# Windowed attention: weighted values by features, softmax weights divided on POOL, transposes in four groups, masks of 32 rows

## The chip, the core and the metric

The kernel runs on one core of a Trainium2 chip. Its engines work side by side, each on its own queue of instructions: TensorE (PE) multiplies matrices and loads their stationary operands (PEld), VectorE (DVE) and ScalarE (ACT) do element work and read TensorE's results from PSUM, GpSimd (POOL) does element work on SBUF only, and SyncE (SP) starts the DMAs. The metric is the device time of one execution in microseconds, the median of several runs.

## The reference

The input is x of 8 batches of 512 rows and 128 features. A first stage adds to x a normed linear attention (16 heads, squared scores). The second stage, which the change touches, runs six layers of windowed attention and a feed-forward block on the normed x. Cut to what matters:

```python
for i in range(6):
    x = attn_layer(shift_tokens(x), Wqkv[i], q_scale[i], k_scale[i], Wo[i]) + x
    x = ffn_layer(shift_tokens(x), ln_g[i], ln_b[i], W1[i], b1[i], W2[i], b2[i]) + x

def attn_layer(x, Wqkv, qs, ksc, Wo):          # 16 heads of 64
    q, k, v = split(x @ Wqkv, 3)
    q = rotate(l2norm(q) * qs); k = rotate(l2norm(k) * ksc)
    # windows of 32 rows: each row sees its window and the one before it
    sim = bq @ [bk_prev, bk].T * 8, masked
    out = softmax(sim) @ [bv_prev, bv]
    return out @ Wo
```

All data is float32. The masks are bfloat16.

## The kernel before, in words

The 512 rows of a batch are four blocks of 128 rows, each with four windows of 32. A block of a batch in a layer is a *unit*; there are 6 x 8 x 4 = 192. The state of a batch lies in SBUF by features (`state[b]`, 128 features by rows).

The loop over t is a software pipeline: in slot t, unit t is projected, unit t-1 gets its scores, unit t-2 its weighted values, and unit t-3 its output product. The feed-forward block of a batch follows its last block (j = 3) at lags 3 to 6, so the slots with t mod 4 = 2, 3, 0 and 1 hold the norm's transposes (`feed_norm`), the normed transposes (`feed_first`), the hidden layer (`feed_middle`) and the last product (`feed_last`).

The steps of a unit:

- `proj(s)`, s = 0 for q and 1 for k (L409): two matmuls of 512 columns (each runs in two passes) into a PSUM tile `mm` of two banks. DVE multiplies them by the rotary tables (L429 twice, L436), ACT squares them (L444), POOL adds the two products into `qk` (L454), DVE sums the squares per head (L457). `unit_length` makes the inverse root on ACT and multiplies q and k by it on POOL (L470).
- `values` (L474): v's projection into an `mm` tile, copied by ACT (L482); SP's DMAs then bring each window's own and previous 32 rows side by side into `v2`.
- `by_features` (L498): transposes of q and k, two calls of eight (four of q, four of k), into `tr` tiles of one bank each, copied by ACT into `qT` and `kT` (L514). POOL keeps k's last 32 columns for the next block (L517).
- `scores` (L519): two matmuls write the mask into the two banks of `sp` (L527), 64 products of 64 rows by 32 columns add q times k (L534). DVE takes the maximum (L542), ACT sixteen exponentials into `pe` (L546), DVE the sum and its reciprocal (L552, L553).
- `by_keys` (L556): transposes of `pe`, copied by ACT into `pT` (L564).
- `weigh_values` (L566): 64 products with `pT` as the stationary operand (64 rows by 32 columns) and 64 columns of v streamed, into `po` (L574). DVE divides by the sum on the way out, `on` (L582).
- `out_by_features` (L588): eight transposes of `on`, two ACT copies into `oT` (L596). `out_project` (L598): eight products with Wo (L603), which DVE adds to the state (L608).

TensorE runs in the order in which the code issues its work (`manual_schedule` at L694). On the other engines a planner orders the instructions from the code's order, its own costs and `high_priority` marks; `issue_behind(later, earlier)` forces an order on one engine without a wait. PSUM is rotated: `mm` has two buffers of two banks, `tr` two of one bank, and `s` has a single buffer of two banks which `sp` and `po` share in turn. A matmul into a rotated buffer waits for the readers of its previous content.

ACT loads the gelu table at the start of a slot with a hidden layer, behind the previous exponentials (L81), and the table of logarithm and exponential behind the last gelu (L75).

Of the kernel before, what the change touches and what calls it, by code (L numbers as in the profile page):

```python
# [26 lines left out]
def sandwich_kernel(ctx: ExitStack, tc: tile.TileContext, ins: dict, out: bass.AP):  # L27
# [40 lines left out]

    def transposed(ps, src, rows, cols):
        nc.tensor.transpose(ps[:cols, :rows], src, ident[:rows, :rows])  # L70


    tables, exps, divisions = [], [], []
# [7 lines left out]
    def gelu_only():  # L81
        ld = nc.scalar.preload_act_table_set("gelu_and_others")
        issue_behind(ld, exps[-1])
        tables.append(ld)
# [324 lines left out]
    def proj(u, s):  # L409
# [18 lines left out]
        def turned(a):  # L428
            nc.vector.tensor_tensor(  # L429
# [4 lines left out]

        def straight():
            nc.vector.tensor_tensor(  # L436
# [6 lines left out]
        def squared(a):  # L443
            nc.scalar.activation(sq[:, :, a, :], ps[:, a], AF.Square)  # L444

# [3 lines left out]
        squared(0)  # L449
        squared(1)  # L450
        u["sq"] = sq
        if s == 0:
            sum_squares(u, 0)
        nc.gpsimd.tensor_tensor(qk[:, s].rearrange("p h a d -> p a h d"), t1, t2, ALU.add)  # L454

    def sum_squares(u, s):
        su = nc.vector.tensor_reduce(  # L457
            u["ss"][:, s], u["sq"].rearrange("p h a d -> p h (a d)"), AX.X, ALU.add
        )
        if s == 1 and divisions:  # L460
            issue_behind(su, divisions[-1])
# [12 lines left out]
    def values(u):  # L474
# [3 lines left out]
        v0 = f3.tile([P, 2, 512], F32, tag="v0", name="v0")  # L478
        ps = psum.tile([P, 2, 512], F32, tag="mm", name="mm")
        for p in range(2):  # L480
            nc.tensor.matmul(ps[:, p, :], lhs, L["wqkv"][:, 2, p, :], start=True, stop=True)  # L481
        nc.scalar.copy(v0, ps)  # L482
# [15 lines left out]
    def by_features(u, c):  # L498

        j, qk, B_ = u["j"], u["qk"], u["B"]  # L500
        if c == 0:
            u["qT"] = f1.tile([P, NP, P], F32, tag="qT", name="qT")
            if j == 0:
# [3 lines left out]
        for s in range(2):  # L507
            ps = psum.tile([P, 4, P], F32, tag="tr", name="tr")
            for i in range(4):
                h0 = 2 * (c + i)  # L510
                transposed(ps[:, i, :], qk[:, s, h0 : h0 + 2].rearrange("p h a d -> p (h a d)"), P, P)
            dst = u["qT"][:, c : c + 4, :] if s == 0 else u["kT"][:, c : c + 4, W:]
            with tc.high_priority():
                nc.scalar.copy(dst, ps)  # L514
        if c == NP - 4 and j < NB - 1:
# [3 lines left out]
    def scores(u):  # L519
# [4 lines left out]
        mk = mask0 if u["j"] == 0 else mask  # L524
        sp = psum.tile([P, 2, NP, 2 * W], F32, tag="s", name="sp", bufs=1)
        for p in range(2):
            nc.tensor.matmul(  # L527
                sp[:, p], identb, mk.unsqueeze(1).to_broadcast([P, NP, 2 * W]),
# [22 lines left out]
        su = f2.tile([P, NP, 2], F32, tag="su", name="su")  # L551
        nc.vector.tensor_reduce(su, pe, AX.X, ALU.add)  # L552
        nc.vector.reciprocal(su, su)  # L553
        u["pe"], u["su"] = pe, su

    def by_keys(u):  # L556
        pe = u["pe"]
        u["pT"] = pT = f1.tile([P, NP, P], F32, tag="pT", name="pT")
        for c in range(0, NP, 4):
# [3 lines left out]
            with tc.high_priority():  # L563
                nc.scalar.copy(pT[:, c : c + 4, :], ps)  # L564

    def weigh_values(u):  # L566

        v2, pT, su = u["v2"], u["pT"], u["su"]
        po = psum.tile([P, 2, NP, HD], F32, tag="s", name="po", bufs=1)
        for pair in range(NP):  # L570
            for w in range(4):
                for p in range(2):
                    r = slice(HD * p, HD * (p + 1))
                    nc.tensor.matmul(  # L574
                        po[W * w : W * (w + 1), p, pair, :],
                        pT[r, pair, W * w : W * (w + 1)],
                        v2[r, w, HD * pair : HD * (pair + 1)],
                        start=True, stop=True,
                    )
# [251 lines left out]
```

## Time and profile before

| | |
|---|---|
| median of 3 runs | 3899.24 us (3893.05 to 3900.62) |
| the profiled execution | 3893.85 us |
| its span, first to last instruction | 3892.1 us |
| first stage (before the first slot of the loop over t) | about 535 us of the span |
| PE busy, mean granted clock | 3729.8 us (96%), 0.99 |
| DVE, ACT, POOL busy | 72%, 68%, 47% |
| DMA, mean share of 16 engines by queue | 22.4% + 0.9% + 0.1% |

A line of the page's groups reads: line of the kernel, engine, operation, output <- inputs, shape, count | busy us, mean ns of one | idle before it and what ended it. A line in order of time reads: start us, duration us, engine, line, operation, how many merged, and in brackets the idle time before it and its releaser. A line by windows reads: the window and its length, then for each engine the busy us and the number of instructions, the granted TensorE clock, the DMA share and GB/s. PE durations include the pipeline's latency, so starts, not durations, give the rate of matmuls.

### The profile page before, as it was taken

What the parts mean: (1) busy time and instruction counts of PE and PEld (TensorE: products, weight loads), DVE (VectorE), ACT (ScalarE), POOL (GpSimd) and SP (SyncE); (2) the same over time, 40 slices, a digit from 0 to 9 for tenths busy, and PEclk for the clock granted to TensorE, in tenths of its full rate; (3) what the DMA queues carried; (4) which work ended last, traced back from release to release, by engine and by line L of the source; (5) the groups of instructions that cost most, each with busy time, mean ns of one, the idle gap of its engine ahead of it and who ended that gap; (6) DMA issues with size and microseconds to landing.
All of it is one profiled execution on the core that took longest, in us unless ns stands there. A gap on an engine that the chain in (4) does not pass through costs nothing.

```text
span 3892.1 us, 149565 instructions
## 1 busy us (share of the span) xinstructions
PE 3729.8 (96%) x65600; PEld 2474.2 (64%) x65600; DVE 2818.2 (72%) x4300; ACT 2657.5 (68%) x6745; POOL 1837.0 (47%) x1311
## 2 busy tenths in 40 slices
PE   8999989999999999999999999999999999999997
PEld 4555456666666666666666666666666666666665
DVE  4555567777867777777777777777787777777775
ACT  5565656776767777777777677777677777766664
POOL 0000025555555555555555555555555555555552
PEclk9999999999999999999999999999999999999998
DMA  2000012222222222222222322223222222222221
GB/s 81 17 9 12 6 50 71 59 66 60 76 74 63 63 63 66 71 75 65 60 62 64 82 65 66 65 56 82 70 66 59 66 65 56 65 68 68 64 67 37
DMA packets 153208, 233.46 MB, mean 60 GB/s; under 512 B 32622, under 2 KB 53356, under 8 KB 151788
## 3 DMA queue, kind: packets, MB, share of 16 engines
q1 hardware_dynamic: 152556, 223.89, 22.4%
q8 instruction: 517, 8.47, 0.9%
q14 instruction: 135, 1.11, 0.1%
HBM read 24.54 MB, written 4.19 MB: 7 GB/s over the span
## 4 chain that ended last, share of the span: by engine, by line
PE 89%; ACT 5%; issue 3%; DVE 2%; DMA 0%; POOL 0%; POOLq 0%; DVEq 0%; SPq 0%; ACTq 0%
PE tr L70 17%; PE mm L421 17%; PE mm L481 9%; PE py L603 9%; PE sp L534 7%; PE po L574 6%; PE y L282 4%; PE mm L625 3%; PE py L657 3%; PE mm L626 3%; PE sc L252 2%; PE sp L527 2%; ACT sq L444 2%; PE vv L230 2%; PE po L318 2%
## 5 line engine op out<-in xcount | busy, mean ns | idle before, releaser
L454 POOL TENSOR_TENSOR qk<-t,t 128x1024 f32<-128x1024 f32 x384 | 909.2, 2368 | 999.6 <-DVE t L436 999.5
L421 PE MATMUL mm<-wqkv,state 128*128 128x512 f32 x1536 | 727.1, 596 | 3.7 <-ACT v L482 2.6
L470 POOL TENSOR_TENSOR qk<-qk,ss 128x1024 f32<-128x1024 f32 x384 | 722.3, 1902 | 16.0
L429 DVE TENSOR_TENSOR t<-mm,tab 128x512 f32<-128x512 f32 x768 | 497.8, 685 | 242.8 <-PE mm L421 231.3
L546 ACT ACTIVATE pe<-sp,mx 128x64 f32<-128x64 f32 x3072 | 651.4, 376 | 27.6 <-DVE mx L542 27.3
L436 DVE TENSOR_TENSOR t<-mm,tab 128x1024 f32<-128x1024 f32 x384 | 465.9, 1213 | 0.0
L457 DVE TENSOR_REDUCE ss<-sq 128x16 f32<-128x1024 f32 x384 | 461.9, 1203 | 2.0 <-ACT sq L444 2.0
L444 ACT ACTIVATE sq<-mm 128x512 f32<-128x512 f32 x768 | 422.6, 610 | 47.2 <-DVE t L436 45.6
L603 PEld LDWEIGHTS py<-oT,wo 128*128 128x128 f32 x3072 | 374.8, 193 | 93.5 <-issue 56.2
L70 PEld LDWEIGHTS tr<-ident,qk 128*128 128x128 f32 x3072 | 345.7, 141 | 127.1 <-issue 105.7
L70 PE MATMUL tr<-ident,qk 128*128 128x128 f32 x3072 | 412.1, 277 | 7.4 <-ACT qT L514 2.3
L596 ACT COPY oT<-tr 128x512 f32<-128x512 f32 x384 | 207.3, 589 | 266.2 <-PE tr L70 265.2
L421 PEld LDWEIGHTS mm<-wqkv,state 128*128 128x128 f32 x1536 | 264.1, 192 | 191.6 <-issue 188.0
L481 PE MATMUL mm<-wqkv,state 128*128 128x512 f32 x768 | 367.9, 602 | 16.8 <-ACT sq L444 16.8
L603 PE MATMUL py<-oT,wo 128*128 128x128 f32 x3072 | 376.0, 276 | 1.0 <-ACT oT L596 0.9
L582 DVE TENSOR_TENSOR on<-po,su 128x1024 f32<-128x1024 f32 x192 | 235.1, 1224 | 170.1 <-PE po L574 170.1
L534 PEld LDWEIGHTS sp<-kT,qT 64*32 64x32 f32 x24576 | 271.9, 106 | 116.7 <-issue 113.8
L574 PE MATMUL po<-v,pT 64*32 64x64 f32 x24576 | 299.3, 225 | 44.7 <-issue 44.7
L482 ACT COPY v<-mm 128x1024 f32<-128x1024 f32 x192 | 194.5, 1013 | 211.0 <-PE mm L481 211.0
L534 PE MATMUL sp<-kT,qT 64*32 64x64 f32 x24576 | 312.2, 227 | 26.0 <-issue 25.2
L574 PEld LDWEIGHTS po<-v,pT 64*32 64x32 f32 x24576 | 258.5, 105 | 86.4 <-issue 86.2
L542 DVE TENSOR_REDUCE mx<-sp 128x16 f32<-128x1024 f32 x192 | 234.6, 1222 | 106.9 <-PE sp L534 106.3
(108 smaller groups left out, 5171.0 us busy)
## 6 DMA issues: line engine op xcount, KB each, us to landing
v<-v SPq DMA_DIRECT2D x1152, 128.0 KB
v<-v SPq DMA_DIRECT2D x672, 64.0 KB
wqkv<-in_L_ffn_Wqkv_dram SPq DMA_DIRECT2D x6, 1536.0 KB
wo<-in_L_ffn_Wo_dram SPq DMA_DIRECT2D x6, 512.0 KB
xin<-_attn_hidden_states_dram SPq DMA_DIRECT2D x8, 256.0 KB
xr<-_attn_hidden_states_dram SPq DMA_DIRECT2D x8, 256.0 KB
x<-xr SPq DMA_DIRECT2D x8, 256.0 KB
xr<-x SPq DMA_DIRECT2D x8, 256.0 KB
```

The lines of the kernel that those rows point to most:

```text
L70: nc.tensor.transpose(ps[:cols, :rows], src, ident[:rows, :rows])
L421: nc.tensor.matmul(ps[:, a].rearrange("p h d -> p (h d)"), lhs, wqkv[:, s, a, :], start=True, stop=True)
L429: nc.vector.tensor_tensor(t2[:, a], ps[:, 1 - a], tab[:, 2 * s + 1, j, HF * a : HF * (a + 1)].unsqueeze(1).to_broadcast([P, H, HF]), ALU.mult,
L436: nc.vector.tensor_tensor(t1, ps, tab[:, 2 * s, j, :].rearrange("p (a d) -> p a d", a=2).unsqueeze(2) .to_broadcast([P, 2, H, HF]), ALU.mult,)
L444: nc.scalar.activation(sq[:, :, a, :], ps[:, a], AF.Square)
L454: nc.gpsimd.tensor_tensor(qk[:, s].rearrange("p h a d -> p a h d"), t1, t2, ALU.add)
L470: nc.gpsimd.tensor_tensor(t, t, ss[:, i, :].unsqueeze(2).to_broadcast([P, H, HD]), ALU.mult)
L481: nc.tensor.matmul(ps[:, p, :], lhs, L["wqkv"][:, 2, p, :], start=True, stop=True)
L534: nc.tensor.matmul(sp[W * w : W * (w + 1), p, pair, :], qT[HD * p : HD * (p + 1), pair, W * w : W * (w + 1)], kT[HD * p : HD * (p + 1), pa ...
L546: ex = nc.scalar.activation(pe[:, pair, p, :], sp[:, p, pair, :], AF.Exp, bias=mx[:, p, pair : pair + 1])
L574: nc.tensor.matmul(po[W * w : W * (w + 1), p, pair, :], pT[r, pair, W * w : W * (w + 1)], v2[r, w, HD * pair : HD * (pair + 1)], start=Tru ...
L603: nc.tensor.matmul(py, L["wo"][:, c, :], oT[:, c, :], start=(c == 0), stop=(c == NP - 1))
```

## The change

Four things change in the second stage.

1. *Weighted values by features.* In `weigh_values` v is now the stationary operand (64 rows by 64 columns) and 32 columns of `pT` are streamed, so the result comes out with features on the partitions. The transposes and copies of `out_by_features` go; one ACT copy of 128 x 1024 makes `oT`. The rows of Wo are put into the matching order before the launch.
2. *Division on POOL.* A new step `shares`, two slots behind the projection, sums the exponentials in two halves on DVE and multiplies the weights themselves by the reciprocals on POOL, before `by_keys` transposes them.
3. *Order.* `by_features` now does four transposes per call, of q or of k; the first two calls come ahead of `values`, `by_keys` comes after it, the third call before `weigh_values` and the fourth after. `values` is issued in halves, of which ACT copies one and DVE the other. Squares, sums of squares and additions become steps of their own, and new `issue_behind` edges order them: the first squares behind the exponentials, q's and k's copies behind the first squares, the second squares behind q's second copy, the second projection's products behind the half sums, the additions behind the division. The gelu table is loaded behind the copies of `by_keys`.
4. *Masks of 32 rows.* For all but a batch's first block, the mask product takes 32 rows, with a fourfold identity `each` as the stationary operand; the two banks' products use different rows of the array.

```diff
+    each = const.tile([2 * W, P], BF16, tag="each", name="each")
+    for a in range(2):
+        for w in range(4):
+            nc.vector.tensor_copy(
+                each[W * a : W * (a + 1), W * w : W * (w + 1)], ident[W * a : W * (a + 1), W * a : W * (a + 1)]
+            )
...
-        issue_behind(ld, exps[-1])
+        issue_behind(ld, pcopies[-1])
...
+            if s == 1 and sums:
+                issue_behind(t, sums[-1])
...
-        squared(0)
-        squared(1)
...
+    def squared(u, s):
+        sq, ps = u["sq", s], u.pop(("psum", s))
+        for a in range(2):
+            q2 = nc.scalar.activation(sq[:, :, a, :], ps[:, a], AF.Square)
+            if s == 0 and exps:
+                issue_behind(q2, exps[-1])
+            if s == 1 and "cp" in u:
+                issue_behind(q2, u["cp"])
         if s == 0:
-            sum_squares(u, 0)
-        nc.gpsimd.tensor_tensor(qk[:, s].rearrange("p h a d -> p a h d"), t1, t2, ALU.add)
+            qsquares.append(q2)
+
+    def add_turned(u, s):
+        t1, t2 = u.pop("parts")
+        add = nc.gpsimd.tensor_tensor(u["qk"][:, s].rearrange("p h a d -> p a h d"), t1, t2, ALU.add)
+        if divisions:
+            issue_behind(add, divisions[-1])
...
-        if s == 1 and divisions:
-            issue_behind(su, divisions[-1])
+        if s == 0:
+            issue_behind(su, u["straight"])
...
-        for p in range(2):
-            nc.tensor.matmul(ps[:, p, :], lhs, L["wqkv"][:, 2, p, :], start=True, stop=True)
-        nc.scalar.copy(v0, ps)
+        nc.tensor.matmul(ps[:, half, :], lhs, L["wqkv"][:, 2, half, :], start=True, stop=True)
+        if half == 0:
+            nc.scalar.copy(v0[:, 0], ps[:, 0])
+            return
+        nc.vector.tensor_copy(v0[:, 1], ps[:, 1])
...
+        with tc.high_priority():
+            cp = nc.scalar.copy(dst, ps)
+        issue_behind(cp, qsquares[-1])
+        u["cp"] = cp
...
+            r = slice(W * p, W * (p + 1))
+            lhs, mk = (identb, mask0) if u["j"] == 0 else (each[r], mask[r])
             nc.tensor.matmul(
-                sp[:, p], identb, mk.unsqueeze(1).to_broadcast([P, NP, 2 * W]),
+                sp[:, p], lhs, mk.unsqueeze(1).to_broadcast([lhs.shape[0], NP, 2 * W]),
...
-        su = f2.tile([P, NP, 2], F32, tag="su", name="su")
-        nc.vector.tensor_reduce(su, pe, AX.X, ALU.add)
-        nc.vector.reciprocal(su, su)
...
+    def shares(u):
+
+        pe = u["pe"]
+        for c in range(0, NP, 4):
+            part = pe[:, c : c + 4].rearrange("t c p k -> t (c p) k")
+            su = f2.tile([P, NP], F32, tag=f"su{c}", name="su")
+            red = nc.vector.tensor_reduce(su, part, AX.X, ALU.add)
+            if sums:
+                issue_behind(red, sums[-1])
+            rc = nc.vector.reciprocal(su, su)
+            sums.append(rc)
+            with tc.high_priority():
+                dv = nc.gpsimd.tensor_tensor(
+                    part, part, su.unsqueeze(2).to_broadcast([P, NP, 2 * W]), ALU.mult
+                )
+        divisions.append(dv)
...
-        po = psum.tile([P, 2, NP, HD], F32, tag="s", name="po", bufs=1)
-        for pair in range(NP):
+        po = psum.tile([P, 2, NP // 2, P], F32, tag="s", name="po", bufs=1)
+        for k in range(NP // 2):
             for w in range(4):
...
+                for i in range(2):
+                    for p in range(2):
+                        r, c, o = slice(HD * p, HD * (p + 1)), 2 * k + i, HD * (i ^ p)
+                        nc.tensor.matmul(
+                            po[o : o + HD, p, k, W * w : W * (w + 1)],
+                            v2[r, w, HD * c : HD * (c + 1)],
+                            pT[r, c, W * w : W * (w + 1)],
+                            start=True, stop=True, skip_group_check=True,
+                        )
+        u["oT"] = oT = f1.tile([P, 2, NP // 2, P], F32, tag="oT", name="oT")
         with tc.high_priority():
...
+            nc.scalar.copy(oT, po)
...
+            at(t, 0, proj, 0)
+            at(t, 3, out_project)
+            at(t, 0, squared, 0)
+            at(t, 2, shares)
+            at(t, 0, add_turned, 0)
+            at(t, 0, proj, 1)
+            at(t, 0, add_turned, 1)
+            at(t, 0, sum_squares, 0)
...
+            at(t, 1, by_features, 0, 0)
+            at(t, 1, by_features, 0, 1)
+            at(t, 0, values, 0)
+            at(t, 0, values, 1)
+            at(t, 2, by_keys)
             if gelus:
                 gelu_only()
...
+            at(t, 1, by_features, 4, 0)
+            if 0 < t < len(units):
+                units[t]["cp"] = units[t - 1]["cp"]
+            at(t, 0, squared, 1)
             at(t, 2, weigh_values)
             at(t, 0, sum_squares, 1)
             if not gelus:
                 at(t, 0, unit_length)
-            at(t, 1, by_features, 4)
+            at(t, 1, by_features, 4, 1)
...
-            at(t, 2, out_by_features)
```

## The prediction

> **What bounds the kernel now.** I read the page first (busy shares and the chain that ended last), then the busy time slot by slot, then one slot in order of time. "Slot" is one turn of the loop over t; its start is the first matmul of `proj(0)`. From the page, the shares and the chain:
>
> ```profile
> PE 3729.8 (96%) x65600; PEld 2474.2 (64%) x65600; DVE 2818.2 (72%) x4300; ACT 2657.5 (68%) x6745; POOL 1837.0 (47%) x1311
> PE 89%; ACT 5%; issue 3%; DVE 2%; DMA 0%; POOL 0%; POOLq 0%; DVEq 0%; SPq 0%; ACTq 0%
> ```
>
> TensorE is the bound and its waits are few. Busy time in four slots in a row, t mod 4 = 0, 1, 2, 3 (window, length, engines):
>
> ```profile
> 2168.59:2189.37 20.78, 20.78 (x331) 12.80 (x331) 13.53 (x18) 15.45 (x37) 7.30 (x7) 0.92 0.23 59
> 2189.37:2206.84 17.47, 16.82 (x326) 11.40 (x325) 12.74 (x17) 11.05 (x32) 12.34 (x9) 1.00 0.16 40
> 2206.84:2221.43 14.59, 14.59 (x325) 10.76 (x323) 12.09 (x23) 11.45 (x34) 7.11 (x6) 1.00 0.38 99
> 2221.43:2238.05 16.62, 15.32 (x324) 10.97 (x323) 13.96 (x20) 11.15 (x32) 9.73 (x7) 1.00 0.26 65
> ```
>
> Over the 48 slots of each kind the medians between starts are 19.81, 16.77, 14.87 and 15.73 us: they differ by the feed-forward piece (hidden layer, last product, transposes of the norm, of the normed). 192 slots fill 3275 of the 3892 us. The third slot in order of time (start, duration, what):
>
> ```profile
> 2206.19 1.23 DVE L542 TENSOR_REDUCE mx<-sp 128x16 f32<-128x1024 f32 x1 [0.61 <-PE sp L534]
> 2207.56 3.39 ACT L546 ACTIVATE pe<-sp,mx 128x64 f32<-128x64 f32 x16
> ...
> 2210.04 1.21 DVE L436 TENSOR_TENSOR t<-mm,tab 128x1024 f32<-128x1024 f32 x1
> ...
> 2211.34 1.09 ACT L444 ACTIVATE sq<-mm 128x512 f32<-128x512 f32 x2 [0.39 <-DVE t L436]
> ...
> 2212.06 1.04 PE L70 MATMUL tr<-ident,pe 128*128 128x128 f32 x8
> ...
> 2212.70 1.08 ACT L564 COPY pT<-tr 128x512 f32<-128x512 f32 x2 [0.27 <-PE tr L70]
> ...
> 2215.62 1.49 PE L574 MATMUL po<-v,pT 64*32 64x64 f32 x128
> ...
> 2217.14 1.23 DVE L582 TENSOR_TENSOR on<-po,su 128x1024 f32<-128x1024 f32 x1 [0.41 <-PE po L574]
> ...
> 2218.42 0.59 PE L527 MATMUL sp<-mask,identb 128*128 128x512 bf16 x2
> ...
> 2218.95 1.62 PE L534 MATMUL sp<-kT,qT 64*32 64x64 f32 x128
> ...
> 2220.50 1.09 PE L70 MATMUL tr<-ident,on 128*128 128x128 f32 x8
> ```
>
> The reader should see TensorE's pieces lying end to end, and two facts that matter below: the division (`on`) of 1.23 us lies under eight transposes and the norm's before the masks reuse its PSUM banks, and the last eight transposes (2220.50) stand between the scores and the next slot, so that the maximum and the start of the exponentials lie under them.
>
> **What the Trainium skill says.** "TensorE: Matmul & The Clock Gate", section LDWEIGHTS: a load costs its columns over 1.2 ns, rows do not count; 64 columns are 53 ns. The trace agrees: in the sums L212 (N=4, so only the loads matter) sixteen pairs of 128 columns start 0.112 us apart. "TensorEngine Tiling (Array Packing)", Key Properties: different tiles load and multiply in parallel, a change of mode drains. The trace agrees: L252 records eight 128-column loads in 0.42 us, where in turn they would take 0.89. "PSUM — Partial Sum Buffer", Terms: two engines may not be on one bank at once, reads included. So squares follow the DVE products of the same projection: the 0.39 us wait at 2211.34.
>
> ```profile
> 94.05 1.95 PE L212 MATMUL vs<-cb,tw 128*128 128x4 f32 x16 [0.16 <-ACT tqk L222]
> ...
> 319.26 0.42 PEld L252 LDWEIGHTS sc<-tqk 32*128 32x128 f32 x8
> ```
>
> **The change part by part**, per slot, starts read from the third slot.
> - Output transposes go: eight at 0.109 us, 0.87 us of TensorE, and two ACT copies of 0.59; one ACT copy of 128x1024 comes (`v` L482: 1.01 us).
> - Masks of 32 rows: two 0.216 us matmuls in separate row groups run together: -0.22 us, in three slots of four (first blocks keep the old mask).
> - Weighing: still 128 loads and 128 matmuls, but loads of 64 columns on four tiles instead of 32 columns on eight. Now: 1.27 us at best (start 2215.62, last about 1.27 later), 1.42 to the next piece. After: half of 0.112 is 0.056 us per load and tile, 32 rounds = 1.79 us; +0.5. Bounds: 1.27 (loads hide) and 2.64 if a tile can't load while it multiplies (0.056+0.027, 32 rounds). I take 1.79: in the old burst eight tiles issue in 0.056 us with a 64-column matmul each, so loads hide there.
> - Division leaves DVE (1.23) for POOL: two multiplies of 128x512, each half of L470's 1.90, say 1.0. Two half sums (0.68 each, as L429's 512 elements) and two reciprocals replace 1.22+0.24. POOL goes from about 9.1 to 11.1 us per slot; cover: it is idle after its two unit-length multiplies, which now end about 3.5 us into the next slot, while the q transposes want them at 5.2. After the feed-forward slot it is about 5.1 against 5.66 for k.
> - Half of v's copy moves to DVE, +0.68: DVE stays at 12 of 14.6 us, cover.
> - New orders, and what queues behind: on ACT behind the first squares the q and k copies and half of v's; on DVE behind the half sums the second projection's products (from 6.7; today from 7.48) and then `sum_squares`; on POOL behind the division both additions, 7.95 to 12.7, then the unit length.
> - Eight small copies for `each` at the start and Wo in another row order (same bytes): nothing; the input loads cover them.
> - SP's ten or so v DMAs wait for the later weighing (about 1.4 us later) and for DVE's half copy; their tile is read two slots on: nothing.
>
> Now the order. Times from the slot's start, which is now the end of the scores: projections and `out_project` to 5.22 as now; four groups less two: q, k 5.22 to 6.10; values to 7.82; `by_keys` to 8.75.
> Upstream: maximum 0.1 to 1.32, exponentials 1.5 to 4.84, first squares (put behind them) 4.8 to 5.9; values need that bank pair at 6.10: slack about 0.2. Half sums follow the state adds, 4.94 to 6.65, POOL 5.9 to 6.95 and 6.95 to 7.95; `by_keys`' second half wants it at 8.3: slack 0.3.
> Downstream, where the gain is lost: the second q group reuses the `tr` buffer of `by_keys`' first half, whose copy runs 8.46 to 9.04 (0.64 after the transposes begin, as at 2212.06 and 2212.70): TensorE waits 0.35, starts at 9.10, weighs 9.7 to 11.5. Second squares, behind q's copy, end at 11.3; the `oT` copy runs 11.7 to 12.7. Second k group and norm transposes end at 12.4, and the masks need the banks that `oT` frees: 12.77, another 0.4. Masks and scores then take 2.08-0.22 = 1.86: slot 14.63.
>
> Fourth kind: the maximum falls behind the norm's DVE pieces (in the fourth slot it started 0.40 after the slot's start, long after its scores); that pushes values by some 0.6: 15.3. Second kind: 11.95+2.58+0.06+1.86 = 16.45. First kind: old masks or not, the gelu table load (1.28) now sits before q's second copy and the second squares, whose bank the hidden layer takes: 0.6 lost, 19.65. Against the medians: -0.16, -0.32, -0.24, -0.43, together -1.15 per four slots, times 48 = -55 us. The weighing also starved for instructions (PE waits of 44.7 us in 62 cases inside it); slower tiles let the queue fill, so I credit 15 of these. Sum -70: span 3892 to 3822. The runs' median stands 7 us over that span (3899.24; the profiled execution took 3893.85), hence **3829**.
>
> **The rivals.**
> *Deeper gain:* weighing stays near 1.3 us, or `oT` goes ahead of the squares. Masks start at about 12.4, and slots two to four gain a further 0.3 to 0.5: about -110 in all, 3785. For it: old loads were hidden. Against: 64 columns against 32 streamed.
> *Slower: the softmax loop becomes the bound.* Scores, maximum, exponentials, squares, values, `by_keys`, weighing, `oT`, masks now form a ring with 0.2 us of slack, as the eight transposes that covered its start are gone and squares and POOL were hung behind the exponentials. If the order on DVE holds the maximum back in every slot by 0.8 us, as it does today in the fourth kind, 0.6 passes to each of 192 slots: +115 on 3829, 3945. It decides at about 0.2 + 70/192 = 0.56 us. For it: DVE is 83% busy. Against: near a slot's end its queue is mostly empty (0.61 idle before the maximum at 2206.19, which waited for the scores alone).
> *Slower by the weighing:* 2.64 us, 0.85 per slot past the `oT` copy, less what first slots absorb: about 3940. Against: the overlapping loads just shown.
> *No difference:* waits eat exactly what the work saves; 3899.
>
> **How the numbers follow.** Likeliest 0.50 (own range 3795 to 3865), deeper 0.15, softmax ring 0.22, weighing 0.08, none 0.05. Faster 0.65, same 0.05, slower 0.30; 0.2% is about what a measurement of this kernel can tell from no change. The range runs from 3775, which leaves a slice of the deeper case out, to 3955, past both slower cases' centres.
>
> **What would show it.** Weighing at about 1.8 us per slot (14 ns a matmul); masks waiting for the `oT` copy; q's second group waiting for the `pT` copy; squares right behind exponentials with values close after; POOL near 60% busy. It is wrong if values or `by_keys` wait for ACT or POOL in most slots, if the weighing is at 1.3 or 2.6, or if the ACT queue holds `oT` behind other copies.

## The result, and the profile after

The changed kernel takes 4150.16 us (median of 4 runs, 4145.27 to 4156.73), the kernel before 3899.8 us beside it: a ratio of 1.0647, interval 1.0626 to 1.0668. It is 250 us slower where the prediction had it 70 us faster. Its profiled execution has a span of 4144.5 us against 3892.1, so 252 us are to be found in the trace.

The page of the changed kernel, shares and chain:

```profile
PE 3784.5 (91%) x64064; PEld 2439.9 (59%) x64064; DVE 2779.7 (67%) x4692; ACT 2581.7 (62%) x6558; POOL 2219.9 (54%) x1695
PE 79%; ACT 12%; DVE 4%; issue 4%; DMA 0%; POOL 0%; POOLq 0%; ACTq 0%; DVEq 0%; SPq 0%
```

TensorE runs 1536 fewer matmuls (the transposes of `on`) and yet is busy 55 us longer; it is idle 360 us where it was idle 162; and 12% of the chain is now on ACT, which had 5%. TensorE is still the bound, but it now waits more often, and part of that is for ACT.

Busy time in four slots in a row of the changed kernel, t mod 4 = 0, 1, 2, 3 (window, length, then PE, PEld, DVE, ACT, POOL, granted clock, DMA share, GB/s):

```profile
2277.67:2297.95 20.28, 19.37 (x330) 11.83 (x322) 13.39 (x19) 14.32 (x33) 10.02 (x9) 1.00 0.31 81
2297.95:2317.30 19.35, 17.11 (x323) 11.19 (x317) 12.63 (x18) 11.34 (x33) 14.03 (x11) 1.00 0.11 26
2317.30:2333.28 15.98, 14.96 (x320) 10.68 (x315) 12.66 (x26) 11.02 (x32) 9.30 (x8) 1.00 0.34 88
2333.28:2352.56 19.28, 16.32 (x319) 11.29 (x315) 12.90 (x21) 10.40 (x30) 11.85 (x9) 0.91 0.24 58
```

The third slot, the shortest kind, now has 1.0 us in which TensorE does nothing; before it had none. The fourth is not typical: it holds 3.4 us of a granted clock of 0.50, and a stop of TensorE of which more below. Medians between starts over the 48 slots of each kind are 20.29, 18.39, 16.01 and 16.73 us; before, 19.81, 16.77, 14.87 and 15.73. Every kind lost, from 0.5 to 1.6 us, so the cause is to be sought in what every slot does.

The granted clock is lower too: 0.982 over the span against 0.990, and 0.979 to 0.983 in all four runs. Stretches with a granted clock of 0.50 sum to 92 us inside the slots after and to 34 before. My estimate from these two figures: if TensorE loses half of each stretch, they cost 46 and 17 us, so up to 29 of the 242 us that the slots lost. Why less clock was granted was not tested.

The third slot in order of time (start, duration, what, and in brackets the idle time before it and what ended that):

```profile
2318.86 3.38 ACT L574 ACTIVATE pe<-sp,mx 128x64 f32<-128x64 f32 x16 [4.64 <-DVE mx L570]
...
2322.01 1.20 ACT L462 ACTIVATE sq<-mm 128x512 f32<-128x512 f32 x2
...
2323.49 1.02 PE L502 MATMUL mm<-wqkv,state 128*128 128x512 f32 x2
...
2324.55 0.58 ACT L504 COPY v<-mm 128x512 f32<-128x512 f32 x1 [0.22 <-PE mm L502]
...
2325.19 1.13 PE L502 MATMUL mm<-wqkv,state 128*128 128x512 f32 x2 [0.68 <-ACT v L504]
...
2326.16 1.04 PE L77 MATMUL tr<-ident,pe 128*128 128x128 f32 x8
...
2326.79 1.07 ACT L606 COPY pT<-tr 128x512 f32<-128x512 f32 x2 [1.65 <-PE tr L77]
...
2327.43 0.66 PE L77 MATMUL tr<-ident,qk 128*128 128x128 f32 x4 [0.24 <-ACT pT L606]
...
2328.02 2.07 PE L618 MATMUL po<-pT,v 64*64 64x32 f32 x128
...
2330.15 1.01 ACT L626 COPY oT<-po 128x1024 f32<-128x1024 f32 x1 [0.45 <-PE po L618]
...
2331.22 0.39 PE L555 MATMUL sp<-mask,each 32*128 32x512 bf16 x2
```

In the third slot of the kernel before, the values were one burst without a wait:

```profile
2212.94 1.88 PE L481 MATMUL mm<-wqkv,state 128*128 128x512 f32 x4
```

Read the new slot against the predicted times. Values start at 6.19 us from the slot's start (predicted 6.10); the squares end at 5.91 (5.9) and the division at 8.15 (7.95). But between the two halves of the values stand 0.68 us in which TensorE waits for ACT's copy of the first half, and the transposes of `pe` begin at 8.86 instead of 7.82. From there on the pieces come in the order and at the distances predicted, 1.0 to 1.15 us late: the weighing from 10.72 (predicted 9.7) to 12.6, `oT` at 12.85 (11.7), the masks at 13.92 (12.77). Masks and scores then take 2.06 us where 1.86 were laid out.

The waits of the changed kernel (who waited for whom: total us, times, longest; PE is the matmul, PEld the load of its stationary operand, whose recorded wait begins earlier):

```profile
PEld mm L502 <- ACT v L504: 290.7, 192, 2.8
...
PE mm L502 <- ACT v L504: 131.0, 192, 2.0
...
PEld tr L77 <- ACT pT L606: 90.1, 190, 0.5
...
PE po L618 <- issue: 62.1, 43, 3.7
...
PE tr L77 <- ACT pT L606: 45.2, 189, 0.2
```

192 times, once a slot, the second half of the values waits for L504. None of the waits forecast as dangerous (squares, division, ring of the softmax) is among TensorE's large ones. The values' and the weighing's waits before:

```profile
PE mm L481 <- ACT sq L444: 16.8, 46, 2.2
...
PE po L574 <- issue: 44.7, 62, 2.1
```

"issue" means that TensorE stood still and the profile shows nothing that it waited for. The traces do show where such stops fall. The page lists the queues that bring instructions (queue, packets, MB, share of 16 engines), here of the changed kernel and of the kernel before:

```profile
q8 instruction: 505, 8.27, 0.9%
...
q8 instruction: 517, 8.47, 0.9%
```

505 packets are one for every 256 of TensorE's 129235 recorded instructions. Counted in order of start (matmuls, loads, semaphore instructions), the stops of over 0.5 us between two starts inside the weighing or the scores lie, to within one instruction, a multiple of 256 instructions apart. That holds for all 68 after, all 79 before and all 819 in the thirteen traces of this case, and TensorE goes on 1.2 to 1.8 us after a packet of q8 has landed. So these are stops for lack of instructions.

To see the whole difference I cut each of the 191 intervals between one `proj(0)` and the next into TensorE's pieces, each from its first matmul to the first of the next piece, so that a wait counts to the piece before it. Totals in us:

| piece | before | after | E1 | E9 | E6 |
|---|---|---|---|---|---|
| values | 337.7 | 517.2 | 337.5 | 333.9 | 359.0 |
| weighing | 325.0 | 455.1 | 451.9 | 372.9 | 405.5 |
| transposes of `on` | 186.7 | 0 | 0 | 196.1 | 0 |
| transposes of `pe` | 188.4 | 241.6 | 251.2 | 251.0 | 190.8 |
| transposes of q, k | 387.4 | 403.4 | 403.1 | 390.9 | 371.8 |
| masks | 100.1 | 71.9 | 72.1 | 73.4 | 71.3 |
| norm's transposes (both) | 44.2 | 67.1 | 67.9 | 83.9 | 65.2 |
| `proj` | 665.2 | 687.9 | 683.2 | 664.1 | 688.6 |
| scores | 322.1 | 337.7 | 334.3 | 341.2 | 332.5 |
| all slots | 3275.4 | 3517.4 | 3333.3 | 3445.6 | 3209.4 |

(The feed-forward's and the output product's pieces make up the rest; E1, E9 and E6 are experiments below.) The slots lost 242 us: values +180, weighing +130, transposes of `pe` +53, four smaller ones +77, the rest +17; against them -187 for the transposes of `on` and -28 for the masks. Of the weighing's +130, about 111 us are its clean length (1.85 us from the first to the last start where it was 1.27, medians of the slots; "clean" means without a stop), the others longer stops.

### The profile page after: what moved, and what is told of

Its sections match the earlier page's. It is cut to its first block, busy times and chain, and to the rows that moved or that the text cites. A ratio compares the mean times of both kernels' runs of the same rounds, so it can differ in the third digit from the quotient of the medians.

```text
span 4144.5 us, 148218 instructions
## 1 busy us (share of the span) xinstructions
PE 3784.5 (91%) x64064; PEld 2439.9 (59%) x64064; DVE 2779.7 (67%) x4692; ACT 2581.7 (62%) x6558; POOL 2219.9 (54%) x1695
## 4 chain that ended last, share of the span: by engine, by line
PE 79%; ACT 12%; DVE 4%; issue 4%; DMA 0%; POOL 0%; POOLq 0%; ACTq 0%; DVEq 0%; SPq 0%
PE mm L428 13%; PE tr L77 11%; PE po L618 10%; PE mm L502 10%; PE py L633 7%; PE sp L562 6%; PE y L289 4%; ACT pe L574 3%; PE mm L655 3%; PE py L687 3%; PE mm L656 3%; ACT v L504 3%; ACT pT L606 3%; PE sc L259 2%; PE vv L237 2%
## 5 line engine op out<-in xcount | busy, mean ns | idle before, releaser
L428 PE MATMUL mm<-wqkv,state 128*128 128x512 f32 x1536 | 749.0, 610 | 6.7 <-issue 5.0
L593 POOL TENSOR_TENSOR pe<-pe,su 128x512 f32<-128x512 f32 x384 | 392.4, 1042 | 633.6 <-DVE su L590 618.5
L502 PE MATMUL mm<-wqkv,state 128*128 128x512 f32 x768 | 420.2, 629 | 145.3 <-ACT v L504 131.0
L77 PE MATMUL tr<-ident,qk 128*128 128x128 f32 x3072 | 456.8, 282 | 53.4 <-ACT pT L606 45.0
L618 PE MATMUL po<-pT,v 64*64 64x32 f32 x24576 | 412.5, 221 | 62.1 <-issue 62.1
L462 ACT ACTIVATE sq<-mm 128x512 f32<-128x512 f32 x768 | 435.9, 646 | 15.2 <-DVE t L446 14.5
L618 PEld LDWEIGHTS po<-pT,v 64*64 64x64 f32 x24576 | 386.6, 136 | 97.4 <-issue 97.4
L606 ACT COPY pT<-tr 128x512 f32<-128x512 f32 x384 | 206.5, 589 | 321.2 <-PE tr L77 321.2
L428 PEld LDWEIGHTS mm<-wqkv,state 128*128 128x128 f32 x1536 | 264.2, 192 | 216.1 <-issue 198.1
L562 PE MATMUL sp<-kT,qT 64*32 64x64 f32 x24576 | 326.7, 229 | 23.8 <-issue 22.6
L562 PEld LDWEIGHTS sp<-kT,qT 64*32 64x32 f32 x24576 | 282.6, 107 | 88.9 <-issue 83.8
L502 PEld LDWEIGHTS mm<-wqkv,state 128*128 128x128 f32 x768 | 115.5, 190 | 316.3 <-ACT v L504 290.7
```

Source lines behind the costliest of these rows:

```text
L428: nc.tensor.matmul(ps[:, a].rearrange("p h d -> p (h d)"), lhs, wqkv[:, s, a, :], start=True, stop=True)
L502: nc.tensor.matmul(ps[:, half, :], lhs, L["wqkv"][:, 2, half, :], start=True, stop=True)
L562: nc.tensor.matmul(sp[W * w : W * (w + 1), p, pair, :], qT[HD * p : HD * (p + 1), pair, W * w : W * (w + 1)], kT[HD * p : HD * (p + 1), pa ...
L618: nc.tensor.matmul(po[o : o + HD, p, k, W * w : W * (w + 1)], v2[r, w, HD * c : HD * (c + 1)], pT[r, c, W * w : W * (w + 1)], start=True, ...
```

## The experiments

The theory after the result (A in the expectations): the two halves of v lie in one PSUM tile, and once ACT's copy is issued between the two matmuls, the second matmul waits for that copy although it writes the other bank. That wait costs some 180 us; the rest of the loss is the weighing and the `pT` copy. The rival (B): ACT reaches the copies late because the exponentials and the squares behind them run late, and the wait for v's copy is only where that delay shows. Ratios are each to the kernel before, run on the same chip in the same series; its medians there were 3888.47, 3888.13 and 3883.88 us; a "point" is a hundredth of the ratio, some 39 us. From E5 on, A also says that the wider loads set the pace of the weighing, and C is its rival.

**E1, both halves of v before either copy.** The changed kernel, with:

```diff
         if half == 0:
-            nc.scalar.copy(v0[:, 0], ps[:, 0])
             return
+        nc.scalar.copy(v0[:, 0], ps[:, 0])
         nc.vector.tensor_copy(v0[:, 1], ps[:, 1])
```

> The changed kernel with one thing moved: both halves of v's projection are issued before either half is copied out (ACT still copies one, DVE the other). Theory A (the second half's matmul waits for ACT's copy of the first, 0.84 us and a restart in each of 192 slots): the pieces of v's projection fall from 517 to about 340 us in all, and the time falls by 150 to 190, to 3960 to 4000 us. Theory B (the ring through the exponentials and squares is the bound): the wait only moves on, and the time falls by less than 60.

3962.24 us, ratio 1.019 (1.0175 to 1.0205): 4.6 points below the changed kernel's ratio, some 178 us. The values' piece is back at 337.5 us. A slot of it in order of time:

```profile
2226.49 1.88 PE L502 MATMUL mm<-wqkv,state 128*128 128x512 f32 x4
...
2228.41 0.59 ACT L505 COPY v<-mm 128x512 f32<-128x512 f32 x1 [1.08 <-PE mm L502]
...
2230.13 2.07 PE L618 MATMUL po<-pT,v 64*64 64x32 f32 x128
```

Four matmuls (two halves in two passes each) in 1.88 us without a break, and the weighing begins 3.64 us after the values do, where it was 4.53. A is right on the place and the price. But E1 is still 1.9% slower than the kernel before, so the wait is not the whole story.

**E2, the same wait alone in the kernel before.**

```diff
-        for p in range(2):
-            nc.tensor.matmul(ps[:, p, :], lhs, L["wqkv"][:, 2, p, :], start=True, stop=True)
-        nc.scalar.copy(v0, ps)
+        nc.tensor.matmul(ps[:, 0, :], lhs, L["wqkv"][:, 2, 0, :], start=True, stop=True)
+        nc.scalar.copy(v0[:, 0], ps[:, 0])
+        nc.tensor.matmul(ps[:, 1, :], lhs, L["wqkv"][:, 2, 1, :], start=True, stop=True)
+        nc.vector.tensor_copy(v0[:, 1], ps[:, 1])
```

> The kernel before with one part of the change alone: v's projection in halves, each copied out (ACT, then DVE) before the next is issued. Theory A: 0.84 us and a restart per slot, so 150 to 190 us more than before, 4050 to 4090. Theory B: no ring through POOL and the exponentials exists here, so no more than 40 us, 3940.

4067.65 us, ratio 1.0462 (1.0446 to 1.0478): +180 us in a kernel whose exponentials, squares and weighing are untouched. Its waits:

```profile
PEld mm L482 <- ACT v L481: 289.9, 192, 2.8
```

That is the changed kernel's line almost to the microsecond. E2 also gives half of the copy to DVE, but E1 keeps that half and loses the 180 us. Together they settle that the wait needs none of the change's other parts and costs 180 us in both kernels.

**E4, a shorter softmax in the changed kernel.** The rival's test: if late exponentials hold ACT, halving their instructions should free it.

```diff
-        for pair in range(NP):
+        for pair in range(NP // 2):
...
+        ex = nc.scalar.activation(
+            pe[:, NP // 2 :].rearrange("t c p k -> t p c k"), sp[:, :, NP // 2 :], AF.Exp, bias=mx[:, 0, 0:1]
+        )
+        issue_behind(ex, tables[-1])
```

> The changed kernel with the exponentials of the last four head pairs done in one instruction with a single head's maximum (the other heads' maxima are left out there), which takes about 1.0 us from ACT ahead of the first squares. Theory A: values wait for ACT's copy and not for the squares, so at most 25 us less (from the fourth kind of slot), 4125 to 4150. Theory B: 0.8 us or more per slot, 150 us less, 4000.

4107.68 us, ratio 1.0564 (1.0548 to 1.058): 0.8 points, some 32 us, below the changed kernel (more than the 25 that A allowed, far from B's figure). The values' piece stays at 512.7 us (517.2), and TensorE's wait for v's copy at 131.0 us in 192 cases, so what B needed to shrink did not. B is refuted for that wait. It holds in one kind of slot: the fourth went from 16.73 to 16.01 us (the other medians moved by +0.37, -0.38 and -0.02), and TensorE's wait of the values for the squares, 14.1 us in 39 cases in the changed kernel, fell to 3.2 us in 2.

**E3, the masks of 32 rows alone in the kernel before.**

```diff
+            r = slice(W * p, W * (p + 1))
+            lhs, mk = (identb, mask0) if u["j"] == 0 else (each[r], mask[r])
             nc.tensor.matmul(
-                sp[:, p], identb, mk.unsqueeze(1).to_broadcast([P, NP, 2 * W]),
+                sp[:, p], lhs, mk.unsqueeze(1).to_broadcast([lhs.shape[0], NP, 2 * W]),
```

> The kernel before with the masks of 32 rows alone. Both theories: 0.2 us less in the three slots of four that have them, 25 to 35 us in all, 3865 to 3875. If the two products did not run together, no difference.

3878.51 us, ratio 0.9972 (0.9963 to 0.9981): 10 us, less than expected. The masks' piece fell by 29 us as reckoned, but its neighbours gave most of it back: scores +7, norm's transposes +8, hidden layer +4. Between the full-size pieces and the 64x32 tiles of the scores there is now a third tiling, 32x128, and the pieces before and after the masks are longer; that the change of tiling is why is read from where the time lies and was not tested apart.

**E7, the masks and the gelu table's place in the kernel before.** As E3, and the load of the gelu table behind the copies of `pT` instead of behind the exponentials.

```diff
-        issue_behind(ld, exps[-1])
+        issue_behind(ld, pcopies[-1] if pcopies else exps[-1])
```

> The kernel before with the masks of 32 rows and the gelu table loaded behind the copies of the transposed weights, as in the change, instead of at the slot's start. In the kernel before, v's projection waits 0.47 us for the first squares in each of 48 slots with a hidden layer, because the load is in front of them: 15 to 25 us less than e3_before_masks, about 3855 to 3865. If the load then delays q's and k's copies by as much, no difference to e3.

3855.91 us, ratio 0.9919 (0.9901 to 0.9936): 22 us below E3, as expected; the transposes of `pe` went from 188.3 to 169.6 us. Two small edits of the change, taken alone, make the kernel 0.8% faster.

**E5, weighing by rows again, the rest of E1 kept.** The division stays on POOL; DVE copies `po` to `on`, and the eight transposes and two copies come back.

```diff
+        po = psum.tile([P, 2, NP, HD], F32, tag="s", name="po", bufs=1)
...
+                        pT[r, pair, W * w : W * (w + 1)],
+                        v2[r, w, HD * pair : HD * (pair + 1)],
...
-            nc.scalar.copy(oT, po)
+            nc.vector.tensor_copy(on.rearrange("t c p d -> t p c d"), po)
...
+            at(t, 2, out_by_features)
```

> e1_v_together (v's halves issued together) with the weighted values by rows again: 64x32 stationary tiles of the weights, a DVE copy in place of the old division, eight transposes of the output and two ACT copies ahead of the next slot; the division stays on POOL. Theory A (the wider loads set the weighing's pace): weighing falls by about 125 us in all, the transposes cost about 187 us again, so e5 is 40 to 80 us slower than e1, 4000 to 4040 on the scale of the first comparison. Theory C (the loads are hidden, the weighing was slowed by waits of other kinds): weighing stays near 450 us, and e5 is 150 us or more slower.

4147.21 us, ratio 1.0665 (1.0643 to 1.0686), 185 us above E1: far from A's time, and it is C's time without C's mechanism, as the weighing did not stay near 450 us but fell to 359.4. The experiment measured something else too. Who waited for the tile `on`:

```profile
  ACT oT L635: 399.7, 168
  PE sp L555: 133.1, 92
```

DVE's copy of `po` stood behind the second sum of squares, and in half the slots the masks waited for it: the two norm pieces are 184.7 us against 67.9.

**E9, the same with that queue mended.** As E5, and the second sum of squares is issued behind DVE's copy.

```diff
+        elif ocopies:
+            issue_behind(su, ocopies[-1])
...
+            ocopies.append(nc.vector.tensor_copy(on.rearrange("t c p d -> t p c d"), po))
```

> e5_rows with one edge more: the second sum of squares is issued behind DVE's copy of the weighted values. In e5_rows that copy stood behind the sum (11.44 to 12.66, the copy to 13.80) and the masks waited 1.65 us for it in the slots with a norm's transposes. Theory A: that was the whole excess, so about 115 us less than e5, 4030, and 50 to 80 us above e1: the price of weighing by rows in this order. Theory C (weighing by features is worth more than its transposes): it stays over 100 us above e1.

4062.37 us, ratio 1.046 (1.044 to 1.048): 2.7 points, some 105 us, above E1 and 85 below E5. A's 50 to 80 us are missed; over 100 is C's side. In the table above the weighing by features costs 79 us more than by rows and saves 196 of transposes; both keep the same wait for the `pT` copy. So the weighing by features, which the change is named for, is worth about 100 us in this order, as measured; E9 also stops longer inside the weighing (91.5 us against 59.3) and is granted less clock (0.982 against 0.985), and these can't be taken apart from it. E9 has the masks and the gelu table's place in common with E7; what it has beyond them (the four groups with their new orders, the division on POOL, the DVE copies) leaves it 5.4 points, about 210 us, above E7; by pieces, the transposes of `pe` with the wait for the `pT` copy make 81 of it, and the weighing 50, which is by rows in both and differs by its stops. So what loses lies there, and not in the weighing by features.

**E10, what sets the pace of the weighing.** E1, with 64 columns streamed per matmul instead of 32; each window's result overwrites part of its neighbour's.

```diff
-                            po[o : o + HD, p, k, W * w : W * (w + 1)],
+                            po[o : o + HD, p, k, W * min(w, 2) : W * min(w, 2) + 2 * W],
...
-                            pT[r, c, W * w : W * (w + 1)],
+                            pT[r, c, W * min(w, 2) : W * min(w, 2) + 2 * W],
```

> e1_v_together with the weighing's streamed operand doubled to 64 columns (neighbouring windows' weights are multiplied too, so part of the values is overwritten by a neighbour's), same 128 loads of 64 columns. Theory A (loads set the pace, multiplying hides under them): the weighing's 1.85 us per slot and the time stay, within 20 us of e1. Theory C (load and multiply follow each other on a tile): 0.027 us more per tile and round, 32 rounds, 0.86 us per slot, 150 us more.

Twice the columns, and the 128 matmuls take 1.88 us from first to last start (median of the slots) against 1.85. So the multiplying does not set the pace. The loads do, as the prediction had it, as far as their size tells: 1.85 us are 58 ns for each of 32 rounds on four tiles, where "TensorE: Matmul & The Clock Gate", section LDWEIGHTS, gives an estimate of 53 for 64 columns. Loads of another width on four tiles were not run. The total is 3996.13 us, ratio 1.0294 (1.0276 to 1.0313), 1.0 points above E1 all the same, where A had it within 20 us. The waits say where:

```profile
PE sp L555 <- ACT oT L626: 110.7, 84, 2.0
```

The planner, which goes by its own costs, had ordered the other engines anew: on ACT the `oT` copy now stands behind the inverse root of the norm, 13.25 us into a slot of the third kind instead of 11.97, and the masks wait for it (norm pieces 161 us against 68). The pace is read from the piece, not from the total.

**E6, another order for TensorE.** E1, with the transposes of `pe` in two calls: q's and k's first groups, v's first half, four transposes of `pe`, q's second group, v's second half, the other four, the weighing, k's second group. ACT's second squares go behind the second `pT` copy.

```diff
             at(t, 0, values, 0)
+            at(t, 2, by_keys, 0)
+            at(t, 1, by_features, 4, 0)
             at(t, 0, values, 1)
-            at(t, 2, by_keys)
+            at(t, 2, by_keys, 1)
...
-            at(t, 1, by_features, 4, 0)
-            if 0 < t < len(units):
-                units[t]["cp"] = units[t - 1]["cp"]
+            if 1 < t < len(units):
+                units[t]["cp"] = pcopies[-1]
```

> e1_v_together with another order on TensorE: q's and k's first groups, v's first half, the first half of the weights' transposes, q's second group, v's second half, the second half of the weights' transposes, weighing, k's second group; the second squares behind the second copy of the transposed weights. It takes away the wait of q's second group for the copy of the transposed weights (63 us in e1) by putting other work between. Theory A: 40 to 65 us less than e1, about 3905 to 3920. If POOL's division or the ring through the exponentials bounds the slot, under 15 us less.

3836.73 us, ratio 0.9866 (0.985 to 0.9881): 1.3% faster than the kernel before, 125 us faster than E1, and the fastest measured here. Its page, and the stretch of a slot that was rearranged:

```profile
PE 3695.3 (96%) x64064; PEld 2419.3 (63%) x64064; DVE 2778.1 (72%) x4692; ACT 2565.0 (67%) x6558; POOL 2220.2 (58%) x1695
```

```profile
2174.70 0.60 PE L77 MATMUL tr<-ident,pe 128*128 128x128 f32 x4
...
2175.23 2.07 PE L620 MATMUL po<-pT,v 64*64 64x32 f32 x128
...
2177.36 1.02 ACT L628 COPY oT<-po 128x1024 f32<-128x1024 f32 x1 [0.40 <-PE po L620]
...
2178.43 0.39 PE L555 MATMUL sp<-mask,each 32*128 32x512 bf16 x2
```

With other work between two users of a `tr` buffer no one waits for the `pT` copy: transposes of `pe` 190.8 us instead of 251.2, and the weighing begins 0.53 us after the last four of them without a wait. These 60 us are the gain that was expected. As much again was not: the weighing's piece fell by 46 us at the same clean length of 1.85, as its stops fell from 59.3 us in 43 cases to 20.9 in 23, and the stretches of half clock in the slots from 65 us to 27. Nobody had planned that, so it is luck. q's and k's transposes fell by 31, the values rose by 21. The three moves came together, and what each is worth is not told apart.

**E8, E6 with the `oT` copy shared.** ACT copies one bank of `po`, DVE the other.

```diff
-            nc.scalar.copy(oT, po)
+            nc.scalar.copy(oT[:, 0], po[:, 0])
+            u["oc"] = nc.vector.tensor_copy(oT[:, 1], po[:, 1])
+        ocopies.append(u["oc"])
```

> e6_order with the copy of the weighted values in two halves, one bank by ACT and one by DVE, the second sum of squares behind DVE's half. The masks wait for that copy; two halves of 0.6 to 0.7 us side by side instead of 1.0 us: up to 0.3 us less in the slots where the masks wait, 10 to 40 us less than e6, about 3880 to 3900. If the masks don't wait for the copy, no difference to e6.

3872.97 us, ratio 0.9958 (0.9943 to 0.9974): 36 us slower than E6, a miss. In order of time:

```profile
2198.12 0.59 ACT L631 COPY oT<-po 128x512 f32<-128x512 f32 x1 [0.40 <-PE po L623]
...
2198.74 0.69 DVE L632 COPY oT<-po 128x512 f32<-128x512 f32 x1 [1.35 <-ACT oT L631]
...
2199.48 0.39 PE L558 MATMUL sp<-mask,each 32*128 32x512 bf16 x2 [0.41 <-DVE oT L632]
```

DVE had been idle for 1.35 us and started 0.03 us after ACT's half ended; it waited for that half in all 192 slots. Two engines that read two banks of one tile took turns, 1.31 us in place of 1.02. That looks like the wait of v's halves again, here between two readers; but the two copies also write one tile, `oT`, and which of the two tiles makes them take turns is not told apart.

**E11, E6 with the norm's last DVE pieces behind the maximum.**

```diff
-            nc.vector.tensor_reduce(mx, sp, AX.X, ALU.max, negate=True)
+            maxima.append(nc.vector.tensor_reduce(mx, sp, AX.X, ALU.max, negate=True))
...
+            while norms:
+                for n in norms.pop()():
+                    issue_behind(n, maxima[-1])
```

> e6_order with the four last DVE pieces of the feed-forward norm issued behind the maximum of the scores instead of ahead of it. In the slots with t mod 4 = 3 the maximum starts about 0.7 us late behind them, and v's projection and the masks follow: 15 to 25 us less than e6, about 3815. If those slots have slack elsewhere, no difference to e6.

3852.46 us, ratio 0.9919 (0.9901 to 0.9938), some 20 us slower than E6, a miss: scores +12 and q's and k's transposes +14 us. The maximum did start earlier in the fourth kind (0.11 us into the slot instead of 0.92), but no kind's median fell. 8 us of the loss lie in the fourth kind, and TensorE's wait of the values for the squares grew from 16.5 to 28.6 us. 12 us lie in the second kind, which the edit does not touch. So the earlier maximum brought no gain, and what the edit itself costs is not shown.

## Why the prediction was wrong

The time is 321 us above the forecast of 3829. Some 178 of them are one step, the rest is in the sum.

**The step that failed first: "Half of v's copy moves to DVE, +0.68", taken as cover, and with it "values to 7.82".** It priced the copies on ACT and DVE and never asked what the copy between the two matmuls does to TensorE. The trace shows it: the second half waits in all 192 slots, the piece takes 2.71 us instead of 1.77 (517.2 and 337.7 over 191), and E1 and E2 put 178 and 180 us on it. The prediction had read "PSUM — Partial Sum Buffer", section Terms, as a rule on banks, and v's halves lie in two. But the matmul and the copy share nothing else than the tile, so what this program waits for goes by the tile. The line of before that was quoted for it, ACT's squares waiting for DVE's products, can't tell the two apart, as the last product reads both banks; but a diff that puts a reader between two writes to one tile should have been given a bound from both sides, as the weighing was.

**The sum itself.** Even E1, without that wait, is 74 us above the kernel before, where -70 was forecast. Some terms were nearly right. Removed transposes: 0.87 us by 192 is 167, measured 187. Masks: -0.22 by 144 is -32, measured -28 on the piece. The wait of q's second group for the `pT` copy: 0.35 by 192 is 67, measured 53 to 63. The slots as a whole were too short. Here they are by kind (medians in us; "clean" takes the slots that have no stop of over 0.5 us inside weighing or scores):

| slot | laid out | before | before, clean | E1 | E1, clean |
|---|---|---|---|---|---|
| first | 19.65 | 19.81 | 19.80 | 19.60 | 19.38 |
| second | 16.45 | 16.77 | 16.68 | 17.35 | 17.06 |
| third | 14.63 | 14.87 | 14.73 | 15.11 | 15.09 |
| fourth | 15.3 | 15.73 | 15.12 | 15.78 | 15.64 |

*"Against the medians: -0.16, -0.32, -0.24, -0.43."* A new slot laid out without any stop was set against medians that contain stops. Against the clean slots the same layout gains 0.30 us in four slots and not 1.15: some 41 of the 55 us were never there.

*"slot 14.63", and the second and fourth kind.* E1's clean slots are 0.3 to 0.6 us longer than laid out, and only the first is shorter; together some 55 us. In the third kind three pieces make it: `proj` takes 3.54 us where "as now" meant 3.44; the weighing takes 2.00 to the next piece, as its last start is not its end (1.42 against 1.27 in the prediction's own reading), so that `oT` starts 0.13 later than laid out; and masks and scores take 2.07 and not 1.86. In the second kind there is also a plain slip: the scores in it are those of a batch's first block, so it keeps the old masks (0.52 us where the others have 0.32), and the saving was counted there.

*"slower tiles let the queue fill, so I credit 15 of these".* The stops inside the weighing went from 44.7 us to 59.3 in E1 and to 62.1 in the changed kernel. The credit has the wrong sign: fewer stops, but each is longer, and no run shows a queue that fills.

These three make some 125 of the 144 us between the forecast (-70) and E1 (+74); the rest was not taken apart; the stretch behind the last slot, 11 us longer, and the lower clock are in it.

**What the sum left out.** `proj` +18 us in E1: its first matmul now follows the scores' small tiles directly, which the transposes of `on` did before; with those back (E9) `proj` is at 664.1 again. Norm's transposes +24: in the third and fourth kinds, some 0.25 a slot, the masks wait for `oT`, which was foreseen at 0.4. Scores +12, q's and k's transposes +16. The masks' saving is mostly paid back by their neighbours (E3, 19 of 29 us).

**What held.** The order of the slot, to 0.1 us up to the values and with one shift of 1.0 to 1.15 from there to the masks; a weighing whose pace the streamed columns don't set (1.79 forecast, 1.85 measured; E10); q's second group held by the `pT` copy; POOL's division in time (2.04 us for both halves, predicted 2.0); the chance that values or `by_keys` would be held by ACT as the way to be wrong. The gelu table's new place, charged with 0.6 us in first slots, gained 22 us in 48 of them in the old order (E7); what it does in the new one was not measured apart.

**The rivals.** The softmax ring gave a time and side closer to the result (3945), but not by its mechanism: no piece waits for squares or exponentials in most slots, and E4 took instructions out of that ring for 32 us only, most of them in the fourth kind. Neither the deeper gain nor the slow weighing (2.64 us) came, as the weighing was measured at 1.85. The listed sign that values wait for ACT in most slots did come true, by a cause that no rival had.

**What stays open.** The stops in weighing and scores fall where the next 256 instructions are missing, but what makes them come late in about a quarter of the weighings (43 of 192 in the changed kernel) and why less often in E6's order was not tested; nor was why the granted clock differs between the kernels, nor whether two tiles for v's halves would let the second matmul and ACT's copy overlap.

## What to carry to other kernels

When a diff splits an operation in two, look for what lands between the halves: a reader of a PSUM tile between two writes to it makes the second write wait, here 0.94 us in each of 192 slots, though the two halves lay in two banks. Add up a change as differences of pieces, or compare clean slots with clean slots; a timeline without stalls set against a median with stalls promises a gain that isn't there. And once work has been taken off the bound engine, look at the order of the rest before judging the idea: the same operations cost 1.9% in one order and gained 1.3% in another, though a part of that gain was luck with the stops.

## What the runs showed of the hardware that was not expected

- Two engines on different banks of one PSUM tile took turns: a matmul behind ACT's copy (0.68 us a slot), and in E8 DVE's copy behind ACT's (0.03 us after its end), where the two also write one tile. Both are waits on semaphores in the trace, so the runs show the program's behaviour and leave open what the chip would allow.
- Matmuls with 64-column loads on four tiles start 14.5 ns apart (1.85 us for 128), and nearly the same whether 32 or 64 columns are streamed (1.88).
- In long runs of small matmuls TensorE stops for lack of instructions: all 819 stops of over 0.5 us lie on every 256th instruction, 1.2 to 1.8 us behind the landing of a packet of q8.
- Kernels on one core were granted different clocks: 0.990 before, 0.982 changed, 0.985 in E1, 0.989 in E6 (profiled executions).
- A mask matmul on 32 rows gained 29 us in its own piece and 10 us in the kernel (E3).
